# A graph layer on one core: the uncompacted first block of edges shortened from 112 to 80 units, with two start points moved

## The chip, the cores and the metric

The kernel runs on one core of a Trainium2 chip. The metric is the device time of one execution in microseconds (us), the median of several runs. A core has TensorE (PE) for matrix products, VectorE (DVE), ScalarE (ACT), GpSimd (POOL) and SyncE (SP); SP, ACT and POOL can also issue transfers (DMAs). In this kernel POOL issues the indirect row gathers.

## The reference

The layer takes 12500 nodes with 256 features in float32, and 212500 directed edges, sorted by target (`dst`), each with a source (`src`) and one of 8 types. One edge per node leads from the node to itself (a self-loop), with a type of its own. Cut to what matters:

```python
h = jnp.maximum(_layernorm(x, axis=-1), 0.0)
hx = jnp.einsum('ni,rio->rno', h, weight)            # 8 types
agg = jax.ops.segment_sum(hx[edge_type, src], dst, num_segments=num_nodes)
out = x + agg * 0.5 ** 0.5 + h_bias + (h @ loop_weight) * 0.5 ** 0.5
```

## The kernel before, in words

**Sums first, then weights.** The kernel does not form `hx`. It sums the rows `h[src]` of the edges by target node and type, and then multiplies these sums by the 8 weight matrices. The sums stand in a ring `acc` in SBUF (L365): 2 halves of the features on 128 partitions, 8 types, 768 columns of nodes (6 slots of 128) and a margin.

**Tiles and units.** A tile is 128 rows gathered by one indirect DMA on POOL (`gather`, L918, the DMA at L940), and a unit is two tiles. TensorE multiplies the rows of a tile by a one-hot matrix that VectorE makes for four tiles at once (`onehots`, L997): four matrix records per tile (`edge_sums`, L1035), into one of four PSUM banks. One VectorE addition per unit then adds the bank to the ring (`add_sums`, L1068).

**Two kinds of blocks.** The edges are cut into blocks of at most 128 units, one unit per partition. Block 0 has `RAW` units of 256 edges each, self-loops included, as they stand. Blocks 1 to 6 are compacted: a unit spans 271 edges (`EDGES`), and VectorE steps squeeze out the self-loops so that what is left fits into 256 rows. `prepare(b)` lists a block's steps: reading its edges (L377), source indices (`sources`), the self-loops' types (`last_edges`; its last two steps are `kept`, which makes `loops[b]`, and `begins`, which fills it), the one-hot columns (`columns`) and the places in the ring (`places`). Each removal of `compacted` is a pair of instructions, L456 and L458, and there are 15 pairs in a block. With 112 units, there are 791 units in all and 1581 tiles.

**Node groups.** When the edges of 128 nodes (a group) are all summed, TensorE multiplies their columns of the ring by the weights (`group_work`, L1242, 18 products per group, mixed with the sums), VectorE adds `x` (L1230, L1257), and SP writes the rows out. The slot of the ring is then made ready for the group six further on. For the groups of block 0 it is zeroed by ScalarE (`clear`, L1081). From group index `XG * plan.typed` on, with `XG` = 4, where self-loops are no longer in the tiles, VectorE fills the slot with the node's own row under its self-loop's type: eight instructions per group (`begin`, `own`, L1110). The types come from `mark` (L1131) and `find_types` (L1141 to L1164), once for every four groups. `plan.typed` is 3 before the change.

**Start.** The first tiles gather rows of the input `x`, since `h` is not there yet. VectorE and ScalarE normalise these tiles after they have landed (`batch`, `begin_batch`; L829, L857 to L873 and L839 to L845). At the same time `x` is read, normalised and written to DRAM as `h32` (`norm_rows`, L897). When the last of this is in the program, at tile 28, `norms_end` sets `state["h32"] = t + AHEAD` = 92. From tile `state["h32"] + LATE` = 100 on, `gather` takes rows of `h32`. It waits for all the writes of `h32` once.

**What sets the order.** One Python loop over the tiles writes all queues in program order. Gathers run ahead of the sums: `goal(t)` allows a lead of 64 tiles, which shrinks to 24 after tile 170 and to 8 at the end, and during the start twice the tile's number plus 24. Every gather also waits for the newest unit whose sums stand ahead of it in the program ("no faster than the sums"). From the first tile of four with lead on `h32`, one tile in 28 (`single_rows`) is not gathered by POOL but read row by row by SP and ScalarE (`load_sources`, L969): 50 tiles. The steps of a block are background work: block 1's step k may run from tile `EARLY + k` on, other blocks' from `LOADED + k` after their start, one or more per tile as a credit allows. `mark(q)` does not wait: it runs all steps still needed at once, in place.

Of the kernel before, what the change touches and what calls it, by code (L numbers as in the profile page):

```python
# [28 lines left out]
XG = 4  # L29
# [1 line left out]

EDGES = 271
TURN = 16
RAW = 112
SPAN = TURN * EDGES
BEFORE = 6
WIDE = 312
# [13 lines left out]
SLOTS = 6  # L51
# [38 lines left out]
FIRST = 4  # L90


LATE = 8


PREP = 232
LOADED = 20
EARLY = 44
SETTLE = 4
ROOM = 5  # L100
SHARE = 1.15
# [148 lines left out]
def kernel(  # L250
# [20 lines left out]
    plan = Plan(N, E)  # L271
# [57 lines left out]
    with ExitStack() as main:  # L329
# [28 lines left out]
        outs = [ps_o.tile([P, 2, D], F32, name=f"po{i}") for i in range(2)]  # L358
        msg, oh, offsets, kind = {}, {}, {}, {}
        firsts, stops, loops, marked, typed, gidx, col = {}, {}, {}, {}, {}, {}, {}  # L360
        added, zeroed = {}, {}
        single, fetches = {}, {SP: [], ACT: []}
        counters = [tc.alloc_semaphore(f"rows{i}") for i in range(COUNTERS)]
        fetched, summed = {}, {}
# [74 lines left out]
        def core(got, name):  # L439

            return got[name][:, BEFORE : BEFORE + EDGES]
# [80 lines left out]
        def last_edges(b, got):  # L522

            if b == 0:
                return []

            def selves_():
                nc.vector.tensor_tensor(
                    work_tile(got, "same", 5)[:, :EDGES], core(got, "s"), core(got, "d"),
                    op=ALU.is_equal)  # L530

            def ends():
                nc.vector.scalar_tensor_tensor(
                    work_tile(got, "end", 2)[:, :EDGES], core(got, "rise"), 1.0, got["same"][:, :EDGES],
                    op0=ALU.is_equal, op1=ALU.mult)

            def moves():
                nc.vector.scalar_tensor_tensor(
                    core(got, "rise"), core(got, "d"), firsts[b], line[:, :EDGES],
                    op0=ALU.subtract, op1=ALU.subtract)  # L540

            def codes():
                nc.vector.scalar_tensor_tensor(
                    core(got, "rise"), core(got, "rise"), -2.0 * R, core(got, "t"),
                    op0=ALU.mult, op1=ALU.add)

            def packs():
                nc.vector.scalar_tensor_tensor(
                    packed[:, :EDGES], core(got, "rise"), 1.0, got["end"][:, :EDGES],
                    op0=ALU.add, op1=ALU.mult)  # L550

            def number():
                got["ends"] = small.tile([P, 1], F32, name="number")
                nc.vector.tensor_reduce(got["ends"], got["end"][:, :EDGES], AX.X, ALU.add)
                stops[b] = small.tile([P, 1], F32, name="ends")
                nc.vector.tensor_tensor(stops[b], firsts[b], got["ends"], op=ALU.add)

            def kept():
                nc.vector.tensor_single_scalar(
                    work_tile(got, "kinds", 5, I32)[:, :LASTS], packed[:, :LASTS], 2 * R - 1,  # L560
                    op=ALU.bitwise_and)
                loops[b] = small.tile([P, 2, PLACES + LASTS], BF16, name="loops")
                nc.vector.memset(loops[b][:, 0, LASTS:PLACES], 0.0)
                nc.vector.scalar_tensor_tensor(
                    loops[b][:, 0, :LASTS], line[:, :LASTS], got["ends"], got["kinds"][:, :LASTS],
                    op0=ALU.is_lt, op1=ALU.mult)

            def begins():

                at = small.tile([P, LASTS], I32, name="at")  # L570
                nc.vector.tensor_scalar(
                    at, line[:, :LASTS], firsts[b], float(plan.skew), op0=ALU.add, op1=ALU.add)
                nc.vector.tensor_single_scalar(at, at, TURNS - 1, op=ALU.bitwise_and)
                nc.vector.tensor_copy(loops[b][:, 0, PLACES:], at)
                nc.vector.tensor_scalar(
                    loops[b][:, 1, :], loops[b][:, 0, :], -1.0, None, op0=ALU.mult)

            return [selves_, ends, moves, codes, packs, number,
                    *compacted(got, TB + 1, (EDGES - 1).bit_length(), EDGES), kept, begins]
# [226 lines left out]
        for d in range(0, N, XG * P):  # L806
            k = min(XG, (N - d) // P)
# [314 lines left out]

        def mark(q):

            while any(b not in loops for b in plan.blocks[q]):
                step()
            marked[q] = []
            for k, b in enumerate(plan.blocks[q]):
                m = marks.tile([P, 2, XG * GROUP], BF16, tag=f"mark{k}", name="mark")
                for i, edge in enumerate((firsts[b], stops[b])):  # L1130
                    in_run("marks", nc.vector.tensor_scalar(  # L1131
                        m[:, i, :], line, edge, float(-plan.starts[XG * q]),
                        op0=ALU.subtract, op1=ALU.is_ge), b == plan.blocks[q][-1] and i == 1)
                marked[q].append((b, m))
# [84 lines left out]
        def group_work(g):  # L1219

            d0 = plan.starts[g]
            s0, n = slot(g)
            first_dep = [True]
            final = plan.NG - 1 if plan.NG > SLOTS + 1 else None

            def biased(g):
                q, k = divmod(g, XG)
                n = plan.ends[g] - plan.starts[g]
                rows_ = got["x", q]
                nc.vector.tensor_add(rows_[:n, k, :], rows_[:n, k, :], outs[g % 2][:n, 1, :])  # L1230

            def product(r, c, g=g):
                n = plan.ends[g] - plan.starts[g]
                if (r, c) == (R, 0):
                    got["out", g] = outs[g % 2][:, 0, :]
                if r == R:
                    while ("self", g) not in got:
                        advance(None)
                    lhs, rhs = got["self", g][:, c, :n], wl[:, c, :]
                else:  # L1240
                    lhs, rhs = acc[:, c, r, s0 : s0 + n], w[:, c, r * D : (r + 1) * D]
                i = nc.tensor.matmul(got["out", g][:n], lhs, rhs, start=(r == R and c == 0),  # L1242
                                     stop=(r == R - 1 and c == KC - 1))
                latest["pe"] = in_run(
                    "loops" if r == R else "products", i, r >= R - 1 and c == KC - 1).ins
                if (r, c) == (R, 0) and g < 2:
                    tc.add_manual_dep(i.ins, done["bias"], SYNC_DEP, reason="one engine at a time")
                if r < R and first_dep[0]:
                    first_dep[0] = False
                    tc.add_manual_dep(i.ins, added[plan.last[g]].name, SYNC_DEP, reason="sums complete")  # L1250

            def finish():
                q, k = divmod(g, XG)
                rows_ = got["x", q]
                if g != final:
                    biased(g)
                nc.vector.tensor_add(rows_[:n, k, :], rows_[:n, k, :], got["out", g][:n])  # L1257
                if XG * (q + 2) >= plan.NG or n < P:
                    nc.sync.dma_start(out[d0 : d0 + n], rows_[:n, k, :])
                elif k == XG - 1:  # L1260
                    first = plan.starts[XG * q + shorts(q)]
                    nc.sync.dma_start(
                        out[first : d0 + n].rearrange("(k p) d -> p k d", p=P), rows_[:, shorts(q) :, :])
                b = g + SLOTS
                q, k = divmod(b, XG)
                if b < plan.NG:
                    if q < plan.typed:
                        clear(b)
                    else:
                        begin(b)  # L1270
                if q + 1 >= plan.typed and XG * (q + 1) < plan.NG:
                    if k == XG // 4:
                        load_groups("h", h32, q + 1)
                    if k == XG - 2:
                        mark(q + 1)
                    if k == XG - 1:
                        find_types(q + 1)

            def last():
                done["late"].append((done["tile"] + REST, finish))  # L1280

            work = []
            for r in [R, *range(R)] if g != final else range(R):
                for c in range(KC):
                    work.append((0.55, lambda r=r, c=c: product(r, c)))
            work.append((0.0, last))
            if final is not None and g == final - 1:
                work.append((0.0, lambda: biased(final)))
                for c in range(KC):
                    work.append((0.55, lambda c=c: product(R, c, final)))  # L1290
            return work
# [279 lines left out]
```

## Time and profile before

| what | us |
|---|---|
| median of 3 runs | 1943.65 (1942.04 to 1946.68) |
| the profiled execution, its own time | 1944.0 |
| its span, from the first to the last instruction | 1942.2 |
| PE busy | 1696.5 (87%) |
| POOL busy | 1456.5 (75%) |
| DVE busy | 1304.4 (67%) |
| ACT busy | 156.7 (8%) |

The rows of the profile give, for a group of instructions, the source line, the engine, the operation, output and input tiles, the number, then busy time and mean duration, then the idle time of the engine ahead of them and what ended it. "issue" as the cause means that nothing the profile shows was waited for. A row of the timeline gives start and duration in us, the engine, and in brackets the idle time ahead of it. A row of a table by windows gives a stretch of time, and for each engine its busy time and, in brackets, the number of instructions.

### The profile page before, as it was taken

To read this page: it belongs to the slowest core of one execution; us is meant where nothing else is said; L and a number is where in the kernel's file an instruction comes from. 1 tells how busy PE (TensorE), PEld (TensorE's weight loads), DVE (VectorE), ACT (ScalarE), POOL (GpSimd) and SP (SyncE) were. 2 spreads that over 40 slices of the span, in tenths; PEclk is the share of its full clock that TensorE was granted. 3 is DMA by queue.
4 is the path that set the end of the run, shared out by engine and by line. 5 is a ranking of instruction groups with operands and counts; after the bars stand their busy time and mean duration, and the time that the engine had idled before them with its cause. 6 is when DMAs were issued, how large, how long until landed. Compare 5 with 4: busy or idle time off the path is not lost.

```text
span 1942.2 us, 40543 instructions
## 1 busy us (share of the span) xinstructions
PE 1696.5 (87%) x10161; PEld 1457.2 (75%) x10161; DVE 1304.4 (67%) x3284; ACT 156.7 (8%) x333; POOL 1456.5 (75%) x1557
## 2 busy tenths in 40 slices
PE   2368999999889898989898889998898889899998
PEld 1357898989778787767777678777777777787887
DVE  7868666887666776655677656578466568665652
ACT  6977100000000000000000000000000000000000
POOL 7777777777777777777777777777777777777775
PEclk9669999999999899999999999999999999999999
DMA  9964544544444444444544444434444444444442
GB/s 315 387 216 130 150 135 124 147 142 132 122 141 143 121 141 132 121 130 121 152 131 122 142 130 122 148 113 143 131 120 141 131 123 132 122 141 126 131 121 82
DMA packets 158422, 279.41 MB, mean 144 GB/s; under 512 B 35440, under 2 KB 109190, under 8 KB 158182
## 3 DMA queue, kind: packets, MB, share of 16 engines
q0 software_dynamic: 73488, 200.77, 35.0%
q1 hardware_dynamic: 76648, 72.73, 12.0%
q10 hardware_dynamic: 8046, 3.30, 0.9%
q8 instruction: 80, 1.31, 0.3%
q14 instruction: 160, 1.31, 0.2%
HBM read 251.06 MB, written 25.60 MB: 142 GB/s over the span
## 4 chain that ended last, share of the span: by engine, by line
PE 38%; POOL 22%; DMA 21%; issue 9%; DVE 6%; ACT 3%; SPq 0%; DVEq 0%; POOLq 0%; ACTq 0%
POOL msg L940 22%; PE po L1242 19%; DMA msg<-h,gidx 19%; PE ps L1035 17%; ACT msg L873 1%; DVE acc L1068 1%; DVE stats L829 1%; DMA w<-in_L_gnn_weight_dram 1%; DMA xt<-in_x_dram 1%; PE pt L1092 1%; DVE oh L997 1%; DVE moves L456 0%; DMA h<-xt 0%; ACT acc L1081 0%; ACT xt L873 0%
## 5 line engine op out<-in xcount | busy, mean ns | idle before, releaser
L940 POOL DMA_INDIRECT msg<-h,gidx x1431 | 1359.7, 950 | 436.6 <-issue 366.8
L1035 PEld LDWEIGHTS ps<-oh,msg 128*128 128x128 f32 x6324 | 928.3, 197 | 385.0 <-DMA msg<-h,gidx 257.9
L1035 PE MATMUL ps<-oh,msg 128*128 128x136 f32 (+1 forms) x6324 | 1008.5, 289 | 201.2 <-DMA msg<-h,gidx 132.4
L1242 PE MATMUL po<-w,acc 128*128 128x256 f32 (+1 forms) x3136 | 888.5, 388 | 10.0 <-DVE acc L1068 9.6
L1068 DVE TENSOR_TENSOR acc<-acc,ps 128x352 f32 x791 | 408.9, 517 | 402.7 <-PE ps L1035 394.7
L1242 PEld LDWEIGHTS po<-w,acc 128*128 128x128 f32 (+1 forms) x3136 | 517.9, 193 | 46.9 <-DVE acc L1068 12.2
L1110 DVE SCALAR_TENSOR_TENSOR acc<-types,pt 128x256 f32<-128x256 bf16 x688 | 248.6, 412 | 66.6 <-PE pt L1092 61.1
L997 DVE TENSOR_TENSOR oh<-fixed,cols 128x544 f32<-128x544 f32 x396 | 282.9, 715 | 0.0
L1242 PE MATMUL po<-wl,self_t 128*128 128x256 f32 (+1 forms) x392 | 114.7, 418 | 6.2 <-DVE acc L1068 4.3
L940 POOL DMA_INDIRECT msg<-in_x_dram,gidx x100 | 94.8, 948 | 32.2 <-issue 23.8
L1242 PEld LDWEIGHTS po<-wl,self_t 128*128 128x128 f32 (+1 forms) x392 | 72.7, 207 | 15.0 <-DVE acc L1068 5.6
L1230 DVE TENSOR_TENSOR xr<-xr,po 128x256 f32<-128x256 f32 (+1 forms) x98 | 40.5, 414 | 24.4 <-PE po L1242 18.1
L873 ACT ACTIVATE msg<-msg,shift,rstd 128x256 f32<-128x256 f32 x100 | 50.8, 587 | 6.0 <-DVE stats L837 4.6
L1257 DVE TENSOR_TENSOR xr<-xr,po 128x256 f32<-128x256 f32 (+1 forms) x98 | 41.2, 421 | 10.6 <-PE po L1242 7.3
L1092 PE MATMUL pt<-ident,hr 128*128 128x128 f32 (+1 forms) x196 | 39.1, 283 | 4.7 <-DMA hr<-h 2.5
L1097 DVE COPY self_t<-pt 128x256 f32<-128x256 f32 (+1 forms) x98 | 40.5, 414 | 3.1 <-PE pt L1092 2.9
L456 DVE TENSOR_SCALAR moves<-fixed 128x271 int32<-128x271 int32 (+1 forms) x90 | 40.5, 450 | 1.6 <-DVE acc L1068 0.5
L1164 DVE CAST types<-pt 128x512 bf16<-128x512 f32 x22 | 15.2, 691 | 39.0 <-PE pt L1160 39.0
L458 DVE COPY_PREDICATED fixed<-moves,fixed 128x311 int32<-128x311 int32 (+14 forms) x90 | 38.0, 422 | 3.1
L873 ACT ACTIVATE xt<-xt,shift,rstd 128x256 f32<-128x256 f32 x66 | 33.7, 588 | 10.3 <-DVE shift L870 10.3
L1092 PEld LDWEIGHTS pt<-ident,hr 128*128 128x128 f32 (+1 forms) x196 | 25.6, 152 | 7.4 <-DMA hr<-h 2.7
L829 DVE BATCH_NORM_STATS2 stats<-msg 128x6 f32<-128x256 f32 x79 | 27.3, 410 | 0.6 <-issue 0.6
(168 smaller groups left out, 371.7 us busy)
## 6 DMA issues: line engine op xcount, KB each, us to landing
msg<-h ACTq DMA_DIRECT2D x3200, 1.0 KB
msg<-h SPq DMA_DIRECT2D x3200, 1.0 KB
msg<-h,gidx POOLq DMA_INDIRECT x1431, 4.9
xr<-in_x_dram SPq DMA_DIRECT2D x23, 512.0 KB
hr<-h SPq DMA_DIRECT2D x23, 512.0 KB
out_dram<-xr SPq DMA_DIRECT2D x22, 512.0 KB
xt<-in_x_dram SPq DMA_DIRECT2D x16, 512.0 KB
h<-xt SPq DMA_DIRECT2D x16, 512.0 KB
```

Of the source, the lines that this page charges most:

```text
L456: nc.vector.tensor_single_scalar(m, packed[:, :n], 1 << (bit + k), op=ALU.bitwise_and)
L829: in_run("stats", nc.vector.bn_stats(stats[:n, k, :], row), row is here[-1])
L873: nc.scalar.activation(row, row, AF.Relu, bias=shift[:n, j : j + 1], scale=rstd[:n, j : j + 1])
L940: i = nc.gpsimd.indirect_dma_start(out=msg[t], out_offset=None, in_=table[:, :], in_offset=bass.IndirectOffsetOnAxis(ap=gidx[b][:, at : at ...
L997: j = nc.vector.tensor_tensor(o[:, k : k + v, :i, :width], iota_f[:, :width].unsqueeze(1).unsqueeze(1).to_broadcast([P, v, i, width]), of. ...
L1035: j = nc.tensor.matmul(ps[:, c, first : first + width], m[:, c * P : (c + 1) * P], o[:, :width], start=(i == 0 and c == 0), stop=(end and ...
L1068: i = nc.vector.tensor_tensor(a, a, ps, op=ALU.add)
L1092: in_run("turns", nc.tensor.transpose(pst[:, c, :n], rows_[:n, c * P : (c + 1) * P], ident[:n, :n]), c == KC - 1)
L1097: nc.vector.tensor_copy(got["self", g][:, :, :n], pst[:, :, :n])
L1110: i = nc.vector.scalar_tensor_tensor(acc[:, :, r, s0 : s0 + n], of, float(r + 1), pst[:, :, :n], op0=ALU.is_equal, op1=ALU.mult)
L1242: i = nc.tensor.matmul(got["out", g][:n], lhs, rhs, start=(r == R and c == 0), stop=(r == R - 1 and c == KC - 1))
L1257: nc.vector.tensor_add(rows_[:n, k, :], rows_[:n, k, :], got["out", g][:n])
```

## The change

Three constants change. Block 0 has 80 units (`RAW`). Tiles take `h32` from `state["h32"] - 4` on, which is tile 88 (`LATE`). Block 1's steps may run from tile 30 on (`EARLY`). Two guards are changed with them: `mark` now goes on until `begins` has run and not only `kept`, and the first load of `h` rows by `finish` stands at the slot that exists when `plan.typed` is 2.

```diff
-RAW = 112
+RAW = 80
-LATE = 8
+LATE = -4
-EARLY = 44
+EARLY = 30
...
                 nc.vector.tensor_scalar(
                     loops[b][:, 1, :], loops[b][:, 0, :], -1.0, None, op0=ALU.mult)
+                listed.add(b)
...
         def mark(q):
-            while any(b not in loops for b in plan.blocks[q]):
+            while any(b not in listed for b in plan.blocks[q]):
                 step()
...
                 if q + 1 >= plan.typed and XG * (q + 1) < plan.NG:
-                    if k == XG // 4:
+                    if k == max(XG // 4, SLOTS - XG * q):
                         load_groups("h", h32, q + 1)
```

With these the program has 789 units and 1578 tiles, of which 88 are gathered from `x`, 1440 from `h32` and 50 read row by row. There are still 7 blocks. `plan.typed` is 2, so four more groups are filled by VectorE and four fewer zeroed by ScalarE.

More of the change, by code (lines that the diff above doesn't have):

```diff
@@ L360 @@
         firsts, stops, loops, marked, typed, gidx, col = {}, {}, {}, {}, {}, {}, {}
-        added, zeroed = {}, {}
+        added, zeroed, listed = {}, {}, set()
         single, fetches = {}, {SP: [], ACT: []}
```

## The prediction

> **What bounds the kernel now.** I read first the waits of POOL, then the timeline of its gathers at both ends, then the page's list of groups.
>
> ```profile
> POOL msg L940 <- issue: 390.6, 1280, 0.3
> POOL msg L940 <- PE ps L1035: 57.1, 187, 0.3
> POOL msg L940 <- DVE bound_o L1324: 2.1, 1, 2.1
> ...
> L940 POOL DMA_INDIRECT msg<-h,gidx x1431: 942/947/1286, 130.0 to 1925.1; - x179
> L940 POOL DMA_INDIRECT msg<-in_x_dram,gidx x100: 942/947/1110, 4.7 to 128.8; - x100
> ...
> 4.68 1.11 POOL L940 DMA_INDIRECT msg<-in_x_dram,gidx  x1 [2.05 <-DVE bound_o L1324]
> 1925.12 0.95 POOL L940 DMA_INDIRECT msg<-h,gidx  x1 [0.31 <-issue]
> ...
> L1035 PE MATMUL ps<-oh,msg 128*128 128x136 f32 (+1 forms) x6324 | 1008.5, 289 | 201.2 <-DMA msg<-h,gidx 132.4
> ```
>
> The last column of the waits is the longest single wait. After the first gather, none is above 0.3 us, whatever is named as the cause: POOL issues a gather of 0.95 us, pauses 0.30, and issues the next, from 4.68 us to the end. The 1531 gathers start 1530 intervals apart, (1925.12 - 4.68) / 1530 = 1.2552 us each. TensorE, though busy longer, is the one that waits: 132.4 us for gathers to land, in this group alone. So the time is first gather + number of gathers x 1.2552 + tail.
>
> The Trainium skill, Perfetto Trace Analysis, section "Identifying the Most-Contended Engine", takes occupancy as the measure for GpSimd and calls it a fair measure of the distance to the roofline. By that rule POOL at 75% has a quarter to spare. The even 0.3 us of the waits speaks against it here; what it would make of the time is the third rival below.
>
> **The sum.** The tail is this:
>
> ```profile
> 1926.20 3.59 PE L1035 MATMUL ps<-oh,msg 128*128 128x104 f32 x24
> 1929.23 1.15 DVE L1068 TENSOR_TENSOR acc<-acc,ps 128x352 f32 x2 [0.67 <-PE ps L1035]
> 1930.43 7.17 PE L1242 MATMUL po<-w,acc 128*128 128x256 f32 x32 [0.64 <-DVE acc L1068]
> 1937.64 0.42 DVE L1257 TENSOR_TENSOR xr<-xr,po 128x256 f32<-128x256 f32 x1 [7.27 <-PE po L1242]
> ```
>
> From the last gather's start to the span's end pass 1942.2 - 1925.12 = 17.1 us: landing, the last sums, two additions, the last group's products, one addition, the write.
>
> Units: 80 raw ones take 20480 edges, and (212500 - 20480) / 271 rounds up to 709, so 789 instead of 791. The last unit before held 90 edges, one tile; now it holds 152, two tiles: 1578 tiles instead of 1581. The tiles read row by row stay 50. POOL has 88 + 1440 = 1528 gathers, **3 fewer**: 3 x 1.2552 = 3.77 us. The tail ends in the same order as before, with the last group's 16 products (32 records) behind the last addition. The end's two additions belonged to two units, now the last addition waits for two tiles; between 0.6 us less (half of the row's 1.15) and 0.6 more, I take 0. The first gather's path is not touched.
>
> Profiled execution: 1944.0 - 3.8 = 1940.2. It lies 0.35 above the median of 1943.65, so on the median 1939.9 us, provided that no gather waits. The rest of the working is on that.
>
> **Does the earlier h hold POOL?** The first gather from `h32` waits for all writes of it, and comes 12 gathers earlier.
>
> ```profile
> 101.49 4.77 SPq L897 DMA_DIRECT2D h<-xt  x3
> 113.71 1.50 SPq L1183 DMA_DIRECT2D hr<-h  x1
> 115.00 0.95 POOL L940 DMA_INDIRECT msg<-in_x_dram,gidx  x1 [0.31 <-ACT unused L839]
> ```
>
> Tile 88 starts at 115.00. The last write is issued by 106.26 (101.49 + 4.77). The first read of `h32` needs all of it too, and SP issued it between 113.71 and 115.21. So the writes were down at the latest 0.2 us after the 88th gather would ask, at the earliest right after 106.26, 8.7 us ahead. Up to tile 28 the program is the same instruction for instruction. Cost 0 to 0.2 us; I take 0, as 113.71 is the nearest row.
>
> **VectorE's work is what moves.** Block 1's steps start 14 tiles earlier, and `mark` now comes at the first group's end and runs what is missing in one stretch. The changed program's order shows where: behind the addition of tile 52 stand nine pairs L456/L458 and fifteen other steps before the next addition. VectorE, in order, has queued behind that the additions that free PSUM banks, the one-hots from tile 60 on and the statistics for ScalarE; TensorE waits for these, and gathers wait for TensorE's sums. This is the wait that the change adds.
>
> How much spare do the gathers have? The two tables are matrix records of L1035 and gathers begun by a time; four records make a tile.
>
> ```profile
> 0.00:153.15 153.15, 55.47 (x256) 51.08 (x256) 0.74 0.90 299
> 0.00:157.90 157.90, 56.69 (x264) 52.30 (x264) 0.75 0.89 298
> 0.00:189.40 189.40, 71.46 (x360) 67.02 (x360) 0.78 0.80 266
> ...
> 0.00:165.40 165.40, 121.69 (x129) 0.76 0.87 289
> 0.00:167.90 167.90, 123.58 (x131) 0.77 0.86 287
> 0.00:197.90 197.90, 146.27 (x155) 0.79 0.78 259
> ```
>
> Up to tile 167 the gather's number is the tile's. Gather 128 (the 129th) needs the sums up to tile 63 (256 records): 165.4 - 153.15 = 12.2 us to spare. Gather 130 needs tile 65: 10.0. Gather 154 needs tile 89: 8.5.
>
> Now the load on VectorE ahead of the same tile's addition, changed program minus old, counted from the two orders:
>
> ```profile
> L456 DVE TENSOR_SCALAR moves<-fixed 128x271 int32<-128x271 int32 (+1 forms) x90 | 40.5, 450 | 1.6 <-DVE acc L1068 0.5
> L458 DVE COPY_PREDICATED fixed<-moves,fixed 128x311 int32<-128x311 int32 (+14 forms) x90 | 38.0, 422 | 3.1
> L533 DVE SCALAR_TENSOR_TENSOR end<-rise,same 128x271 f32<-128x271 f32 x1 | 0.5, 502 | 0.0
> L660 DVE SCALAR_TENSOR_TENSOR fit<-far,fit 128x1 f32<-128x1 f32 x4 | 0.7, 182 | 0.1
> L1148 DVE TENSOR_TENSOR of<-pt,line 22x512 bf16<-22x512 f32 x22 | 15.0, 682 | 12.2 <-PE pt L1141 11.7 <-issue 0.3
> L1110 DVE SCALAR_TENSOR_TENSOR acc<-types,pt 128x256 f32<-128x256 bf16 x688 | 248.6, 412 | 66.6 <-PE pt L1092 61.1
> ```
>
> At tile 44: six pairs (6 x 0.872 = 5.2) and six steps of 0.3 to 0.5 us (about 2.7) more: 7.9 us. At tile 68: nine pairs (7.8), 40 steps between L660's 0.18 and L533's 0.50 for the most part (their rows add up to 10.5), two `mark` and two `find_types` instructions (2.3): **20.6 us more**. At tile 98 the excess is back to almost nothing, since the old program has done block 1 by then and had 12 more `x` tiles to normalise. The four extra groups' own rows (32 x 0.412 = 13.2 us) come after that.
>
> What takes it up is VectorE's idle time; these rows are of 105 to 132 us (tiles 28 to 42) and of 10 us stretches:
>
> ```profile
> L869 DVE RECIPROCAL rstd<-rstd 128x8 f32<-128x8 f32 (+1 forms) x3 | 0.6, 189 | 6.1 <-ACT rstd L865 6.1
> L857 DVE TENSOR_TENSOR both<-stats 128x24 f32<-128x24 f32 x3 | 0.6, 184 | 6.1 <-ACT stats L845 6.0
> ...
> 130.00:140.00 10.00, 10.00 (x64) 8.61 (x64) 8.08 (x27) 8.56 (x26) 7.85 (x8) 0.96 0.36 105
> 150.00:160.00 10.00, 7.41 (x50) 6.71 (x49) 9.50 (x29) 7.31 (x17) 7.56 (x9) 1.00 0.70 220
> 180.00:190.00 10.00, 5.67 (x37) 4.80 (x36) 9.47 (x30) 5.24 (x16) 7.57 (x9) 1.00 0.37 108
> 210.00:220.00 10.00, 10.00 (x73) 9.45 (x72) 5.68 (x13) 0.00 (x0) 7.56 (x9) 1.00 0.48 147
> ```
>
> Up to tile 44 VectorE idles 12.2 us waiting for ScalarE, so the first 7.9 us cost nothing. The other 12.7 us meet a VectorE that is busy 8.1 to 9.5 of 10 us (third pair of numbers); it idles about 3.5 us there until tile 68. The sums then lag by about 9 us against 10.0 to spare: hidden, by little. Bounds: 0 if the overlap of neighbouring instructions and TensorE's head start of four banks count, 20.6 - 10.0 = 10.6 us if nothing takes any of it up. I take 0, nearer to the worked lag. Without that cover each us of lag beyond 10 is a us of the time, as POOL never makes up. After 210 us VectorE is busy 5.7 of 10, and the extra own rows and the earlier later blocks find room there.
>
> Other edits cost nothing: 12 fewer normalisations and four fewer clears relieve ScalarE, which no gather waits for; the guards fix order only; SP gets one read of `h` earlier among three, with the same 512 KB.
>
> The stretches also answer a rule that speaks against more VectorE work. The Trainium skill, SBUF — State Buffer, section "SBUF: two separate sides", says that a VectorE operation in a two-port mode keeps GpSimd from writing descriptors, so that its DMA stalls. POOL's nine gathers take 7.56 us with VectorE busy 9.50 and 7.56 with it busy 5.68. No loss to see, so I add nothing; by the rule the extra 13 us of own rows could stretch gathers by at most as much.
>
> **Rivals.**
>
> 1. *The lag is not covered* (slower). Place: gathers 128 to 156. It decides once the sums of tiles 63 to 89 come more than 8.5 to 12 us later than before. Price 0 to 10.6 us, so up to 1939.9 + 10.6 = 1950.5; slower than before from 3.8 us of wait on. For it: VectorE near full at 150 to 190 us, all of the burst in one place, and TensorE itself busy 10 of 10 at 130 to 150 us. Against: idle time ahead of it. Chance 0.16; in its lower half, up to 1944 to 1945, little is lost.
> 2. *h32 is late at tile 88*, for instance because weights and the group's reads share the queues. Bound from the rows: 0.2 us; if the waiting grows by as much as the 1.5 us of the read's issue, 1939.9 + 1.5 = 1941.4. Chance 0.05.
> 3. *The pace is TensorE's*, POOL's 0.3 us being room. Then 3 tiles save 12 of 6324 records of 1008.5 us, 1.9 us: 1941.7. Against: TensorE's waits for landings. Chance 0.05.
>
> That the change does not do what it says is excluded by the orders: 1528 gathers stand there.
>
> **How the numbers follow.** Forecast, chance 0.74: 1939.9 us, with 2 us to either side, as the three runs before lie from 1.6 below to 3.0 above their median: 1937.9 to 1941.9. A measurement of this kernel tells about 0.2% (3.9 us) from no change, so "faster" means below 1939.8, almost the forecast itself: of its 0.74 I give 0.42 to faster and 0.32 to no change. Rivals 2 and 3 give 0.01 to faster and 0.09 to no change. Rival 1 gives 0.01 to faster, 0.06 to no change and 0.09 to slower, for which POOL has to wait 7.7 us (3.8 + 3.9). Together 0.44, 0.47, 0.09. The range takes in rival 1's lower half: 1937.8 to 1944.2.
>
> **What would show it.** 1528 gathers with one interval of 1.255 us and no wait above 0.3 us; the gather of tile 88 at 115.0 us; sums of tiles 63 to 71 some 5 to 10 us later than the tables above, and caught up by 200 us; a tail of 17.1 us. A wait of POOL for sums at 160 to 200 us is rival 1; one at 115 us is rival 2. The forecast is wrong if the mean interval changes, or if the tail grows by a group's products, 18 x 0.39 us.

## The result, and the profile after

The changed kernel takes **1939.77 us** (median of 22 runs, 1938.08 to 1942.02), the kernel before 1942.84 us on the same chip (22 runs, 1941.10 to 1946.68). The ratio is 0.9985, with a 95% interval of 0.9980 to 0.9991: 3.1 us less, between 1.7 and 3.9 us. The forecast was 1939.9 us. The profiled execution has a span of 1938.2 us, against 1942.2 before.

The gathers come first: their groups, then POOL's waits (total, how many, longest), then the timeline of POOL at the two places that matter, all of the changed kernel. Line numbers behind L577 are one higher than before.

```profile
L941 POOL DMA_INDIRECT msg<-h,gidx x1440 | 1367.7, 950 | 439.9 <-issue 374.9
L941 POOL DMA_INDIRECT msg<-in_x_dram,gidx x88 | 83.7, 951 | 28.6 <-issue 23.4
```

```profile
POOL msg L941 <- issue: 398.4, 1306, 0.3
POOL msg L941 <- PE ps L1036: 48.5, 159, 0.3
POOL msg L941 <- ACT msg L874: 2.4, 6, 0.9
```

```profile
4.72 1.11 POOL L941 DMA_INDIRECT msg<-in_x_dram,gidx  x1 [2.10 <-DVE bound_o L1325]
...
113.66 1.27 POOL L941 DMA_INDIRECT msg<-in_x_dram,gidx  x1 [0.30 <-issue]
115.24 0.95 POOL L941 DMA_INDIRECT msg<-h,gidx  x1 [0.30 <-ACT unused L840]
...
164.18 0.95 POOL L941 DMA_INDIRECT msg<-h,gidx  x1 [0.30 <-issue]
166.02 0.94 POOL L941 DMA_INDIRECT msg<-h,gidx  x1 [0.89 <-ACT msg L874]
...
1921.51 0.95 POOL L941 DMA_INDIRECT msg<-h,gidx  x1 [0.30 <-issue]
```

There are 1528 gathers, as worked out. The mean interval is (1921.51 - 4.72) / 1527 = 1.2553 us. The first gather from `h32`, at 115.24, has its usual pause of 0.30 us: it waited for nothing (the gather ahead of it took 1.27 us, not 0.95). Behind the first gather, one pause is longer than usual, 0.89 us at 166.02. It belongs to gather 128, which needs the sums up to tile 63, and the cause that the view names (a normalisation of ScalarE) is not it. The windows show what is. They count the matrix records of `edge_sums` that had begun by a time; first the changed kernel, then the kernel before at the times when it had as many.

```profile
0.00:153.15 153.15, 53.24 (x240) 48.59 (x240) 0.72 0.91 302
0.00:157.90 157.90, 53.24 (x240) 48.59 (x240) 0.72 0.90 301
0.00:165.28 165.28, 57.07 (x256) 52.55 (x256) 0.71 0.88 293
0.00:169.25 169.25, 59.36 (x274) 55.03 (x275) 0.72 0.87 288
0.00:202.75 202.75, 78.00 (x400) 73.52 (x400) 0.76 0.78 257
```

```profile
0.00:159.65 159.65, 57.77 (x274) 53.56 (x275) 0.75 0.89 296
0.00:201.45 201.45, 77.53 (x400) 73.09 (x400) 0.80 0.78 257
```

TensorE stands still at 60 tiles (x240) from before 153.15 until after 157.90. The kernel before had 256 records at 153.15, the changed one has them at 165.28: the sums of tile 63 lag by **12.1 us**. Half way through tile 68 (x274) the lag is 9.6 us, and at tile 99 (x400) 1.3 us. TensorE's own timeline has the cause of the standstill, VectorE's additions, which stand behind the stretch of steps that `mark` runs:

```profile
151.27 0.59 PE L1036 MATMUL ps<-oh,msg 128*128 128x104 f32 x4
158.36 1.22 PE L1243 MATMUL po<-w,acc 128*128 128x256 f32 x2 [6.51 <-DVE acc L1069]
```

VectorE's own timeline has the stretch, from its first step to the next addition, 11.1 us in which no bank is freed. Tile 60 goes into the bank that tiles 52 and 53 had, four units before; their addition is the first of the two at 157.81. The one-hots of tiles 60 to 63 had been made ahead of the stretch, so it is the bank that TensorE waits for:

```profile
145.28 0.72 DVE L998 TENSOR_TENSOR oh<-fixed,cols 128x544 f32<-128x544 f32 x1
...
146.70 0.45 DVE L548 SCALAR_TENSOR_TENSOR fixed<-rise,end 128x271 int32<-128x271 f32 x1
...
157.81 1.13 DVE L1069 TENSOR_TENSOR acc<-acc,ps 128x352 f32 x2
```

So the time is accounted for like this. The last gather starts 1925.12 - 1921.51 = 3.61 us earlier: 3.77 for three gathers, less 0.59 for the one wait, and 0.4 that lies in the other intervals, 0.3 ns in each. The tail is 1938.2 - 1921.51 = 16.7 us, 0.4 less than before. Together 4.0 us by the two profiles, 3.1 by the medians.

### The profile page after: what moved, and what is told of

Same layout as the page of the kernel before. It is cut to its first block, busy times and chain, and to the rows that moved or that the text cites. A ratio compares the mean times of both kernels' runs of the same rounds, so it can differ in the third digit from the quotient of the medians.

```text
span 1938.2 us, 40494 instructions
## 1 busy us (share of the span) xinstructions
PE 1693.9 (87%) x10152; PEld 1455.2 (75%) x10152; DVE 1315.0 (68%) x3304; ACT 136.4 (7%) x290; POOL 1453.3 (75%) x1554
## 4 chain that ended last, share of the span: by engine, by line
PE 37%; DMA 22%; POOL 19%; DVE 9%; issue 9%; ACT 3%; SPq 1%; DVEq 0%; POOLq 0%; ACTq 0%; PEldq 0%
DMA msg<-h,gidx 20%; POOL msg L941 19%; PE po L1243 19%; PE ps L1036 17%; DVE acc L1069 2%; ACT msg L874 1%; DVE oh L998 1%; DVE stats L830 1%; SPq L970 1%; DVE acc L1111 1%; ACT xt L874 1%; DVE moves L456 1%; DMA w<-in_L_gnn_weight_dram 1%; DMA xt<-in_x_dram 1%; PE pt L1093 1%
## 5 line engine op out<-in xcount | busy, mean ns | idle before, releaser
L1111 DVE SCALAR_TENSOR_TENSOR acc<-types,pt 128x256 f32<-128x256 bf16 x720 | 259.6, 414 | 65.5 <-PE pt L1093 55.5
L941 POOL DMA_INDIRECT msg<-in_x_dram,gidx x88 | 83.7, 951 | 28.6 <-issue 23.4
L1258 DVE TENSOR_TENSOR xr<-xr,po 128x256 f32<-128x256 f32 (+1 forms) x98 | 41.2, 421 | 10.6 <-PE po L1243 7.3
L874 ACT ACTIVATE msg<-msg,shift,rstd 128x256 f32<-128x256 f32 x88 | 44.8, 587 | 5.0 <-DVE stats L838 3.4
L1149 DVE TENSOR_TENSOR of<-pt,line 22x512 bf16<-22x512 f32 x23 | 15.7, 682 | 20.7 <-PE pt L1142 20.6
```

Of the source, the lines that this page charges most:

```text
L874: nc.scalar.activation(row, row, AF.Relu, bias=shift[:n, j : j + 1], scale=rstd[:n, j : j + 1])
L941: i = nc.gpsimd.indirect_dma_start(out=msg[t], out_offset=None, in_=table[:, :], in_offset=bass.IndirectOffsetOnAxis(ap=gidx[b][:, at : at ...
L1111: i = nc.vector.scalar_tensor_tensor(acc[:, :, r, s0 : s0 + n], of, float(r + 1), pst[:, :, :n], op0=ALU.is_equal, op1=ALU.mult)
```

## The experiments

The first theory is the prediction's: the time is the number of gathers times POOL's interval, as long as the sums of `edge_sums` do not lag by more than the gathers have to spare. The rivals are these. TensorE sets the pace. The earlier rows of `h32`, or the earlier steps, are the gain. The total of VectorE work counts, not where it stands.

The first four runs were on a chip on which the kernel before itself took 2405.24 us (the slow chip below). Three of them were repeated later, where it took 1943.29, 1943.84 and 1946.11 us in the three series. Every run is compared with the kernel before of its own series. In the table, the lag is that of the sums of `edge_sums` against the kernel before, by the traces, at the tile named; up to tile 99 none is more than 0.4 us larger. The waits are what POOL's pauses between 100 and 200 us had beyond 0.3 us, added up.

| run | gathers | lag, us | waits, us | against before, us | ratio, 95% interval |
|---|---|---|---|---|---|
| changed kernel | 1528 | 12.1, tile 63 | 0.6 | -3.1 | 0.9985, 0.9980 to 0.9991 |
| RAW 112 (e8) | 1531 | 5.5, tile 79 | 0 | +0.3 | 1.0002, 0.9993 to 1.0011 |
| EARLY 44 (e6) | 1528 | 18.8, tile 63 | 6.7 | +3.1 | 1.0018, 1.0009 to 1.0027 |
| EARLY 20 (e12) | 1528 | 9.5, tile 63 | 0 | -3.2 | 0.9981, 0.9972 to 0.9990 |
| EARLY 14 (e7) | 1528 | 12.8, tile 63 | 1.7 | -3.3 | 0.9981, 0.9972 to 0.9990 |
| LATE -20 (e10) | 1527 | 11.7, tile 63 | 3.7 | -0.6 | 0.9996, 0.9987 to 1.0006 |
| SINGLE 26 (e11) | 1523 | 10.8, tile 63 | 0 | -7.8 | 0.9962, 0.9948 to 0.9976 |

### The number of gathers: RAW back at 112

```diff
-RAW = 80
+RAW = 112
```

> The changed kernel with RAW back at 112; LATE -4 and EARLY 30 stay. 1531 gathers (88 from x, 1443 from h32), and block 1's steps no longer pile up in one stretch at the first group's end. Theory (POOL's pace times the number of gathers, and a short wait of 0.6 us behind the burst of VectorE steps): 3 x 1.2552 = 3.8 us back, the wait of 0.6 us gone, so 1939.8 + 3.8 - 0.6 = 1943.0 us, the same as before within 0.2%; no POOL wait above 0.3 us after the first gather. Rival (the gain comes from the earlier rows of h or the earlier steps): 1939.8 us.

> The changed kernel with RAW back at 112, LATE -4 and EARLY 30 kept, as in the run on the slow chip: 1531 gathers, no stretch of VectorE steps behind tile 52. Theory (the number of gathers is all of the gain): 1531 gathers at 1.2552 us and no wait, so the kernel before within 0.7 us (ratio 1.000). Rival (the earlier rows of h or the earlier steps are the gain): 3 to 4 us below the kernel before (0.998).

On the slow chip the ratio was 1.0006 (0.9981 to 1.0031). There POOL itself waited, up to 7.6 us at a time, so none of the four runs there tests its pace. On the other it was **1.0002** (0.9993 to 1.0011): with 1531 gathers nothing is gained, though `h32` is used from tile 88 and block 1 starts at tile 30. POOL never pauses longer than usual:

```profile
POOL msg L941 <- issue: 397.4, 1303, 0.3
POOL msg L941 <- PE ps L1036: 49.4, 162, 0.3
```

The gain comes with the shorter block 0, not with the two start points.

### TensorE's pace: half of the products left out

```diff
-            for r in [R, *range(R)] if g != final else range(R):
+            for r in [R, *range(1, R, 2)] if g != final else range(1, R, 2):
```

> The changed kernel with the products of four of the eight types left out (types of even number; the output lacks their share), so TensorE issues 1568 product records fewer, some 489 us less of work; 1528 gathers as before. Theory (POOL's pace): only the tail shrinks, by half of the last group's 7.17 us, so 3.6 us less than the changed kernel, about 7 us less than the kernel before; POOL's interval stays 1.255 us. Rival 3 of the prediction (TensorE's pace): several hundred us less, as POOL's gathers follow the sums more closely and its 0.3 us pauses vanish.

This leaves out the products of the four even types. It takes 1935.96 us against 1943.29 before, **7.3 us less** (0.9954 to 0.9976), where TensorE's pace would have given hundreds. The page's busy times of this run:

```profile
PE 1536.7 (79%) x8584; PEld 1283.8 (66%) x8584; DVE 1311.9 (68%) x3304; ACT 136.1 (7%) x290; POOL 1451.7 (75%) x1554
```

The products' group of this run, then that of the changed kernel:

```profile
L1243 PE MATMUL po<-w,acc 128*128 128x256 f32 (+1 forms) x1568 | 491.4, 399 | 18.8 <-DVE acc L1069 18.8
```

```profile
L1243 PE MATMUL po<-w,acc 128*128 128x256 f32 (+1 forms) x3136 | 888.7, 389 | 8.7 <-DVE acc L1069 8.3
```

The products' busy time falls by 397 us (not the 489 of the expectation), TensorE's whole busy time by 157 (from 1693.9): its other instructions took longer, the sums 311 ns each in place of 289, at a lower granted clock (last section). Its wait for gathers to land doubles, in this run first and in the changed kernel second (total, number, longest):

```profile
PE ps L1036 <- DMA msg<-h,gidx: 255.9, 395, 4.1
```

```profile
PE ps L1036 <- DMA msg<-h,gidx: 122.9, 211, 2.9
```

Its last gather starts at 1919.23 us, 2.3 us ahead of the changed kernel's 1921.51, and no gather waits; the rest is the tail, 14.8 us in place of 16.7. Rival 3 has fallen. The chain of waits in the changed kernel's page would have misled here; it gives TensorE 37% and POOL half of that:

```profile
PE 37%; DMA 22%; POOL 19%; DVE 9%; issue 9%; ACT 3%; SPq 1%; DVEq 0%; POOLq 0%; ACTq 0%; PEldq 0%
```

### The lag and its limit: EARLY at 44, 20 and 14

```diff
-EARLY = 30
+EARLY = 44
```

> The changed kernel with EARLY back at 44: same 1528 gathers. The stretch of VectorE steps behind tile 52 grows from 13.8 to 20.1 us, and none of it is taken up by idle time ahead of it; ahead of tile 68's addition there is 5 us less work than with 30. Theory (rival 1 of the prediction, lag not covered): TensorE stands still some 6 us longer at tile 60, POOL waits for sums at gathers 126 to 132 by 5 to 7 us in all, 1939.8 + 5 to 7 = 1945 to 1947 us. Rival (only the total by tile 68 counts): 5 us less lag, no wait, 1939.2 us.

> The changed kernel with EARLY back at 44, as in the earlier run whose chip ran every kernel some 460 us slower and so told nothing of this: stretch of VectorE steps behind tile 52 of 20.1 us in place of 13.8, no earlier work for the idle time. Theory (rival 1 of the prediction, lag not covered): TensorE stands still some 6 us longer at tile 60, POOL waits for sums at gathers 126 to 132 by 5 to 7 us in all, so the time is 1 to 4 us above the kernel before. Rival (only the total by tile 68 counts, 5 us less than with 30): no wait, 3.5 us below the kernel before.

On the slow chip: 1.0010 (0.9983 to 1.0037), which tells nothing. On the other **3.1 us slower than before**, and so 6 us behind the changed kernel, which was 3.1 faster than before in its own series. The timeline of POOL:

```profile
162.20 0.94 POOL L941 DMA_INDIRECT msg<-h,gidx  x1 [0.30 <-issue]
169.66 0.94 POOL L941 DMA_INDIRECT msg<-h,gidx  x1 [6.52 <-ACT rstd L866]
...
172.66 0.94 POOL L941 DMA_INDIRECT msg<-h,gidx  x1 [0.81 <-ACT msg L874]
```

The window up to the 256 records of tile 63's sums:

```profile
0.00:171.90 171.90, 57.15 (x256) 52.85 (x256) 0.71 0.85 281
```

The sums of tile 63 come at 171.90, 18.8 us later than before, and POOL loses 6.2 + 0.5 us at gathers 126 and 128. The last gather is 1927.89, 6.4 us behind the changed kernel's. This is rival 1 in full, and it makes the whole change slower than the kernel before.

```diff
-EARLY = 30
+EARLY = 20
```

> The changed kernel with EARLY 20, between 14 (four waits of POOL at 148 to 162 us, 1.7 us in all) and 30 (one wait at 166 us, 0.6 us). Theory (the lag at each tile decides, and the load should come as early as idle time takes it, but not into the time when TensorE itself is full at 130 to 150 us): waits of 0 to 0.6 us in all, 0 to 0.6 us below the changed kernel, 3.1 to 3.7 below the kernel before. Rival (the same load always costs the same): about 1 us of waits, between the two.

The window up to tile 63's sums, and the row of POOL's waits for sums:

```profile
0.00:162.60 162.60, 56.85 (x256) 51.65 (x256) 0.71 0.86 285
```

```profile
POOL msg L941 <- PE ps L1036: 51.3, 168, 0.3
```

With a lag of 162.60 - 153.15 = 9.5 us no gather waits. The time is 3.2 us below the kernel before (1.9 to 5.4), which does not stand apart from the changed kernel's 3.1: 0.6 us is less than these measurements can tell, and only the traces show it.

```diff
-EARLY = 30
+EARLY = 14
```

> The changed kernel with EARLY 14 in place of 30: same 1528 gathers, block 1's steps start 16 tiles earlier and no longer stand in one stretch behind tile 52; ahead of tile 68's addition stands about as much VectorE work as with 30. Theory (the lag is what VectorE's early idle time of 12.2 us could not take up, and the stretch makes it worse): the sums of tiles 61 to 67 come some 5 us earlier than with 30, no POOL wait above 0.3 us, 1939.8 - 0.6 = 1939.2 us. Rival (the total of VectorE work by tile 68 counts, wherever it stands): the wait of 0.9 us at 166 us stays, 1939.8 us.

> The changed kernel with EARLY 14, as in the run on the slow chip: block 1's steps start 16 tiles earlier, no stretch behind tile 52, about the same total of VectorE work ahead of tile 68's addition (20.0 us more than the kernel before, against 18.5 with 30). Theory (what counts is the lag at a tile, load less the idle time it meets, and 12.2 us of idle time lie early): sums of tiles 61 to 67 earlier by some 4 us than with 30, no POOL wait above 0.3 us at 160 to 175 us, 0.6 us below the changed kernel, 3.7 us below the kernel before. Rival (only the total counts): the wait of 0.6 us stays, 3.1 us below the kernel before.

On the slow chip 0.9966 (0.9941 to 0.9991), on the other 0.9981. The theory's "no wait" **failed**: POOL loses 1.7 us, only elsewhere. Its timeline:

```profile
146.41 0.95 POOL L941 DMA_INDIRECT msg<-h,gidx  x1 [0.30 <-issue]
148.27 0.94 POOL L941 DMA_INDIRECT msg<-h,gidx  x1 [0.91 <-PE ps L1036]
...
151.59 0.94 POOL L941 DMA_INDIRECT msg<-h,gidx  x1 [1.12 <-ACT msg L874]
```

The windows up to the 208 records of tile 51, of this run and then of the kernel before:

```profile
0.00:150.85 150.85, 51.68 (x208) 45.92 (x208) 0.67 0.91 299
```

```profile
0.00:139.70 139.70, 48.18 (x208) 43.79 (x208) 0.72 0.93 315
```

Gather 116, at 151.59, needs the sums of tile 51 (x208). The kernel before had them by 139.70, this one by 150.85, so at tile 51 the lag is already 11.2 us, and gather 116 would have asked at 4.68 + 116 x 1.2552 = 150.3. Steps that start too early meet the tiles sooner. By the traces a better place is between 14 and 30; the times of 14, 20 and 30 do not stand apart. The rival, that the same total costs the same wherever it stands, falls with the four values: about the same load ahead of tile 68 gives waits of 0.6, 0 and 1.7 us with 30, 20 and 14 (VectorE's instructions ahead of that tile's addition take 20.0, 18.8 and 19.3 us more than before), and the smaller load of 44 (14.1 us more), in one stretch, 6.7.

### The write of h: LATE at -20

```diff
-LATE = -4
+LATE = -20
```

> The changed kernel with LATE -20 in place of -4: rows of h from tile 80 on, the earliest the program allows; 80 gathers from x and 1447 from h32, 1527 in all, as one more tile is read row by row. The first gather from h32 now asks at 105.1 us; the writes of h32 are issued until 106.26 us and were shown to be down at the latest at 115.2. Theory: POOL waits there once, 1.2 us for the issue and about as long again as a gather's landing of 4.9 us, 3 to 6 us in all; that also relieves the place at 166 us (0.6 us), and one gather less is 1.3 us: 1 to 4 us above the changed kernel, between 2 us below and 1 us above the kernel before. Bounds: 1.2 to 10 us of wait. Rival (h32 is down earlier, and more room at tile 88 than the prediction's rows could show): no wait above 0.3 us at 105 us, 1.3 us below the changed kernel.

It takes 1945.47 us against 1946.11: 0.6 us less (2.5 less to 1.2 more). The last writes in SyncE's timeline, and the place in POOL's:

```profile
92.10 14.26 SPq L898 DMA_DIRECT2D h<-xt  x6
```

```profile
103.72 0.94 POOL L941 DMA_INDIRECT msg<-in_x_dram,gidx  x1 [0.30 <-issue]
108.62 0.94 POOL L941 DMA_INDIRECT msg<-h,gidx  x1 [3.96 <-issue]
```

Gather 80 would have started at 104.96 and waits until 108.62, 2.3 us after the last write's issue ends (92.10 + 14.26). So `h32` is down by 108.6 us in this run, and by that the changed kernel's gather 88, at 115.24, has 6.6 us to spare. The lag at tile 63 is nearly that of the changed kernel, but the gathers behind the wait ask later by as much, and none of them waits: the one wait replaces the other.

### Fewer gathers by other means: SINGLE at 24 and 26

```diff
-SINGLE = 28
+SINGLE = 24
```

> The changed kernel with one tile in 24, not 28, read row by row by SyncE and ScalarE: POOL issues 1519 gathers, 9 fewer, while TensorE and VectorE do the same work. Theory (POOL's pace): 9 x 1.2552 = 11.3 us less, 1928.5 us. Rival (TensorE's pace): 1939.8 us, nothing gained. Second rival (the row by row tiles become the late ones): POOL or TensorE waits for them, slower than 1928.5, with waits on their counters.

> EARLY 14 and, besides, one tile in 24, not 28, read row by row: POOL issues 1519 gathers, 12 fewer than the kernel before; TensorE and VectorE do the same work as in the changed kernel. SyncE needs 24 us for its half of a tile, and between two such tiles there are now 24 x 1.255 = 30 us. Theory (POOL's pace): 12 x 1.2552 = 15.1 us below the kernel before, about 1928 us (0.992). Rival (TensorE's pace): 3 to 4 us below the kernel before (0.998). Second rival (SyncE has become the bound, as on the slow chip): slower than the kernel before, TensorE waits for the row by row tiles.

On the slow chip the ratio was 1.0577, on the other (with EARLY 14 besides, e9) **1.0120**, 23 us slower in place of 15 faster. The longest of POOL's waits in e9, and of TensorE's:

```profile
POOL msg L941 <- PE ps L1036: 92.7, 184, 3.3
```

```profile
PE ps L1036 <- PEq L1033: 189.4, 41, 12.2
```

TensorE now waits 189.4 us at line 1033, where it waits for the counters of the tiles that are read row by row, 41 times; with 28 it was this:

```profile
PE ps L1036 <- PEq L1033: 6.2, 2, 4.9
```

The sums come late for that, and POOL's pauses grow by 39 us. So this run could not show POOL's pace; e5 and e8 did. Whether SyncE or ScalarE was the late one was not separated.

```diff
-SINGLE = 28
+SINGLE = 26
```

> The changed kernel with one tile in 26 read row by row: 1523 gathers, 5 fewer than the changed kernel, 8 fewer than before. SyncE needs 24 us for its half of such a tile and has 32.6 us in between (35.1 with 28, 30.1 with 24, where POOL lost 39 us to waits). Theory (POOL's pace, SyncE still in time): 8 x 1.2552 = 10.0 us less than before and 0.6 back, 9.4 us below the kernel before (0.995). Rival (SyncE is already late): POOL waits again, with TensorE waiting for the rows' counters, at or above the kernel before.

1938.30 us against 1946.11, **7.8 us less** (4.7 to 10.1): below both kernels (the changed one was 3.1 less), and 1.6 us short of the expectation. No gather waits, but the last products come later. The last gather of this run, TensorE's last sums of this run, and those of the changed kernel:

```profile
1916.85 0.95 POOL L941 DMA_INDIRECT msg<-h,gidx  x1 [0.30 <-issue]
```

```profile
1918.87 4.19 PE L1036 MATMUL ps<-oh,msg 128*128 128x104 f32 x28
```

```profile
1921.46 4.19 PE L1036 MATMUL ps<-oh,msg 128*128 128x104 f32 x28
```

With 26 TensorE begins its last seven tiles 2.0 us after the last gather's start, in the changed kernel at the same time (1921.46 and 1921.51). The tail is 1935.5 - 1916.85 = 18.7 us in place of 16.7: TensorE had not caught up when the gathers ended. Its waits for the counters of the row by row tiles are 27.7 us here, 7 in number, against 6.2 and 2 above; that these are what put it behind was not tried by itself.

## Why the prediction was right

- **The bound, POOL's interval times the number of gathers.** Right, and shown from three sides: with half of TensorE's products gone the time fell by little more than the tail (e5), with 1531 gathers the gain is gone (e8), and with 1523 it is 7.8 us (e11). The Trainium skill (Perfetto Trace Analysis, "Identifying the Most-Contended Engine") calls occupancy a fair measure, for GpSimd, of how close an engine is to roofline. That does not hold here: POOL's instructions fill 1451.7 of 1934.0 us in e5, 75%, and the span still follows POOL's interval.
- **The sum, three gathers, 3.77 us.** Right in size: the span ended 4.0 us earlier, the median 3.1. That the time itself, 1939.77, is 0.1 us from the forecast is in part luck. The forecast started from 1943.65, the median of three runs; from the 1942.84 of all 22, the same sum gives 1939.1.
- **The tail unchanged.** 0.4 us shorter, within the 0.6 allowed. Four further runs with 80 units (e6, e7, e10, e12) have 16.3 to 16.4 us, and the second with 112 (e8) has 17.9 where the kernel before has 17.1, so a part of the gain may lie in the tail; two profiles with 112 units do not settle how much. The sign "18 x 0.39 us" counts one matrix record for each product, where there are two; that it comes near the 7.17 us of the last group's 32 records is chance.
- **The first gather from `h32` waits for nothing.** Right, and with more room than the rows of before could show: 6.6 us by e10. Rival 2 needed `h32` later by more than that.
- **VectorE's load is "hidden, by little".** Nearly: 0.6 us were not. The load of 20.6 us was 20.0 by the traces, and the lag of about 9 us that was worked out at tile 68 was measured as 9.6 there. Its first 7.9 us did cost something: at tile 44 the sums are 2.4 us late already. The step that failed is that only tile 68 was worked: right behind the stretch, at tile 63, the lag is 12.1, against 12.2 to spare. The stretch also stands one unit earlier than the prediction has it, ahead of the addition of tiles 52 and 53, so that TensorE stops at tile 60 for want of a bank and not of one-hots. And the spare was counted to the end of the sums; gather 128 started 0.7 us after that (166.02 against 165.28), so 11.5 us were to be had. The mechanism was rival 1's, at its place, with a price of 0.6 us out of its 0 to 10.6.
- **Rival 1's condition, "more than 8.5 to 12 us".** Right: lags of 5.5 and 9.5 us cost nothing, 12.1 cost 0.6, 18.8 cost 6.7, so 6.7 us more of lag cost 6.1 more. What held it off was the start of the steps at tile 30; with 44 the whole change is 3.1 us slower than the kernel before.
- **Caught up by 200 us.** Right but for 1.3 us. Afterwards the sums are late again, by 12.8 us at tile 200 in the trace. The four extra groups' own rows, the first of them at 203.0 us, run then, as the prediction said; that they are the cause was not tried by itself. No gather waits there: the one of tile 228, at 287.84 us, needs the sums of tile 163, and the last of these records begins at 273.4, 14 us earlier.
- **VectorE's extra own rows do not hold POOL.** Right: 720 in place of 688 leave the gathers as they were, the changed kernel first, the kernel before second:

```profile
200.00:1000.00 800.00, 605.73 (x637) 0.98 0.47 133
```

```profile
200.00:1000.00 800.00, 605.60 (x638) 0.98 0.46 134
```

But "no loss to see" goes by two stretches of 10 us, and other VectorE instructions do go with slower gathers, those of `mark` above all. One such place in the changed kernel:

```profile
295.24 0.48 DVE L1132 TENSOR_SCALAR mark<-line,ends 128x512 bf16<-128x512 f32 x1
295.36 1.18 POOL L941 DMA_INDIRECT msg<-h,gidx  x1 [0.30 <-issue]
```

In the changed kernel's trace 34 gathers overlap one of the 56 instructions of L1132. They take 1.02 us on average, and 13 of them more than 1.0; the other 1494 take 0.95, and 20 of them more than 1.0. That is about 2.6 us of the span, and 2.5 in the kernel before, where 30 gathers overlap 54 of them. So it is in the mean interval already, and the change hardly moves it. That these instructions are what holds the gathers was not tried by itself.

## What to carry to other kernels

An engine at 75% can be the bound: look for the one whose pauses are all alike, and count its instructions; an engine that is busier but waits for it is not the bound. When work on a third engine is moved, work out the lag at every place that the bound engine needs, the largest right behind the moved stretch, not only where the total is largest, and set it against the spare of that same place. Work that is to be hidden should start early enough to meet the idle time that lies ahead (with 44 it came after it), but not so early that it delays the tiles ahead (as with 14, by the traces).

## What the runs showed of the hardware that was not expected

- With half of the products left out, TensorE's granted clock fell: 0.90 of full speed from 200 to 1000 us, against 0.98 in the changed kernel, and its mean product took 399 ns in place of 389. The Trainium skill (TensorE: Matmul & The Clock Gate, "Part 1: The HAM clock gate") says that the gate sets the clock by how busy the array has been of late. This run agrees: TensorE was busy 79% of the span in place of 87%, and the mean granted clock over the run was 0.872, against 0.954 in e6, of the same series. The row of e5:

```profile
200.00:1000.00 800.00, 605.21 (x639) 0.90 0.48 135
```

- On the slow chip the kernel before took 24% longer, though a gather there had its usual 949 ns. There SyncE's row by row reads took 33.08 / 48 = 0.69 us each, in the changed kernel's profile 41.36 / 106 = 0.39, and the chain of waits of the run with RAW 112 there went through SyncE's queue. Why that chip was so is open. The record numbers it 7, as it does the chip of the last series, where the kernel before took 1946.11 us; whether they are one chip is not known. A stretch of SyncE's timeline there, the chain's shares there, and a stretch of the changed kernel's SyncE:

```profile
604.87 33.08 SPq L970 DMA_DIRECT2D msg<-h  x48
```

```profile
SPq 43%; issue 32%; PE 14%; DVE 6%; another core or an unknown queue 2%; ACT 1%; DMA 1%; DVEq 0%; POOL 0%; PEldq 0%; ACTq 0%
```

```profile
1022.72 41.36 SPq L970 DMA_DIRECT2D msg<-h  x106
```

- POOL's mean interval in single profiles without waits lay between 1.2538 us (e5) and 1.2576 (e12). Over 1527 intervals that is 5.8 us, more than the change is worth: the comparison needs many runs on one chip, and the sum needs the interval of its own profile.
